# Attention with a conditioning token: the last query chunk of every even step exchanged and turned instead of scored twice

## The chip, the cores and the metric

The kernel runs on one core of one Trainium2 chip. The metric is the device time of one execution in microseconds (us). The engines have short names in the profile: PE is TensorE (PEld its weight loads), DVE VectorE, ACT ScalarE, POOL GpSimd, SP SyncE, which here only issues transfers.

## The reference

For each of 8 batch entries, x has 512 rows of 512 columns; there are 16 heads of 32 columns.

```python
Q, K, V = heads(x @ Wq.T + bq), heads(x @ Wk.T + bk), heads(x @ Wv.T + bv)
tQ, tK = heads(tokens @ Wq.T + bq), heads(tokens @ Wk.T + bk)   # one token per batch entry
cQ, cK = Q + tQ, K + tK
scores = einsum('bhqd,bhkd->bhqk', cQ, cK) / sqrt(32)
out = einsum('bhqk,bhkd->bhqd', softmax(scores), V)
return x + merge_heads(out)
```

Everything is float32.

## The kernel before, in words

**Steps.** The work is cut into T = 32 steps; step t = 4b + g does four heads (group g) of batch entry b. A step has 512 queries in four chunks of 128 (qc) and 512 keys in four chunks (kc). The main loop (L1122) runs t from 1 to 28; each turn consists of four items, V, q, k and v, numbered i = 0 to 3. The order of every engine's instructions, and of the transfers on the SP queue, is written out by hand: it is the order in which the program emits them (L260).

**Row scores.** `row_max(t, qc)` (L606) computes 128 x 512 scores of one query chunk for four heads: four matmuls of 32 rows side by side in the array (`row_scores`, L633), into four PSUM banks. VectorE reduces them to negated row maxima (L602 or, two banks at once, L644). `denominators` (L668) lets ScalarE take the exponentials, with the maximum as bias, and sum them along the row (L682). In item i of step t this is done for chunk i + 1 of step t + 1, and in the last item for chunk 0 of step t + 2. So in item i = 2 the last chunk (qc = 3) of step t + 1 is done and all its maxima are known; `held()` (L1135) then emits `split_max` (four small GpSimd instructions, L696 to L699, which split the maxima into three bf16 parts) and `turn_max` (L707), one transposing transfer on SP at L712. Its result, maxT, is what the first matmul of the next step reads.

**Two ways to weighted values.** The product with v needs the exponentials with keys on the partitions, while the row scores have queries there.
- Even steps compute the scores a second time, transposed. `exponentials(t, kc)` (L733) adds, in PSUM, the negated maxima (ones times maxT in bf16, L738) and the scores (L741), 512 queries wide, and ScalarE writes their exponentials to the arena (L752). This is done in item i for kc = i.
- Odd steps from 1 to 27 (the list BLOCKED) keep the exponentials of the rows. `exchange(t, half)` (L657) moves them between groups of 32 partitions by 16 transfers of 128 KB, 12 on SP and 4 on GpSimd's queue, and `turn_blocks` (L650) transposes them on VectorE in blocks of 32 x 32, eight instructions L655 a step. The two halves of the exchange of step t + 1 are emitted behind items 0 and 2 of the even step t; the table TURNED places the turns.

**Item V** does `weighted(t - 1)` (L813): the product of the exponentials of the step before with v (`times_v`, L754, matmuls at L763), the spreading of the sums (L800), reciprocals (L810) and `send` (L827), which turns the result on VectorE (L830), multiplies it by the reciprocals and adds the residual on GpSimd. Matmuls with 32 columns of weights run four side by side.

**Items q, k, v** project for the next batch entry. The 512 x 512 products are done by seven half-size products (Strassen and Winograd). In odd steps `four_products` (L517) does four of the seven, ScalarE copies them out, and GpSimd adds (L544, L545). In even steps `three_products` (L547) does the other three, and VectorE adds them on (L556, 557, 558). A product is 16 matmul instructions at L469.

**Order of a pair.** In an odd step PE does, per item, four row scores and then four products (or the product with v); in an even step four second scores, four row scores and three products (or the product with v). The SP queue carries, per pair and in this order: two halves of the exchange (even step), then in the odd step the store of results and the loads of x (i = 1), maxT's transfer (i = 2) and the loads of the residual xr (i = 3). Transposes of x (`turn_x`) run on VectorE in item 0 of even steps. The last three steps have code of their own behind the loop.

Of the kernel before, what the change touches and what calls it, by code (L numbers as in the profile page):

```python
# [12 lines left out]
ALU = mybir.AluOpType  # L13
# [4 lines left out]
def kernel(  # L18
# [39 lines left out]
    P = 128  # L58
# [17 lines left out]
    BLOCKED = list(range(1, T - 4, 2))  # L76

# [136 lines left out]
    def room_for_e(t, kc, pr):  # L214

        if t + 1 in BLOCKED and kc == 0 and pr == 0:
            place[0] = 8
        i = place[0]
        place[0] = (i + 1) % ROOMS
        return arena[:, i, :].rearrange("p (i s) -> p i s", s=S)  # L220

    def rows_kept(t, half):

        a = arena[:, half * HG : (half + 1) * HG, :]
        return a.rearrange("p g (c h s) -> p g c h s", c=2, h=HG)

# [290 lines left out]
    def four_products(n, b, u, dens, small, at):  # L517

        one_, two_ = banks(at), banks(at + 1)
# [24 lines left out]
        nc.gpsimd.tensor_tensor(c1, c1, twice(m1), ALU.add)  # L544
        nc.gpsimd.tensor_tensor(c22, c22, c12, ALU.add)  # L545

    def three_products(n, b, u, dens, small, at):  # L547

        dens()
        one_, two_ = banks(at[0]), banks(at[1])  # L550
        product(n, b, u, 5, one_[:, HS:])
        product(n, b, u, 4, one_[:, :HS])
        small()
        product(n, b, u, 3, two_[:, :HS])
        c1, c12, c2, c22 = parts_of(n, b, u)
        nc.vector.tensor_tensor(c12, one_[:, HS:], c12, ALU.add)  # L556
        nc.vector.tensor_tensor(c2, halves(one_), twice(c22), ALU.add)
        nc.vector.tensor_tensor(c12, two_[:, :HS], c12, ALU.add)
# [47 lines left out]
    def row_max(t, qc, hold=False, w=HG, singly=False):  # L606
# [4 lines left out]
        for j in range(HG):  # L611
            row_scores(t, qc, j, banks(w + j))
# [20 lines left out]
    def row_scores(t, qc, j, pt):  # L633
        r = slice(j * HD, (j + 1) * HD)
        nc.tensor.matmul(  # L635
# [31 lines left out]

    def denominators(t, qc, w=HG, js=range(HG)):  # L668
# [3 lines left out]
        for j in js:  # L672
            if t in BLOCKED:
                to = rows_kept(t, qc // 2)[:, :, qc % 2, j, :].rearrange(
                    "p g (c e) -> p g c e", e=BL
                )
            else:
                to = banks(w + j)
            of = banks(w + j)
            if t in BLOCKED:  # L680
                of = of.rearrange("p (c g e) -> p g c e", g=HG, e=BL)
# [51 lines left out]
    def exponentials(t, kc, at=None):  # L733

        bank = [bank_of(i) for i in at] if at else [banks(i) for i in range(HG)]
        for j in range(HG):
            r = slice(j * HD, j * HD + 3)
            nc.tensor.matmul(bank[j], onesb[r, :], maxT[t][r, :], start=True, stop=False)  # L738
        for j in range(HG):
# [4 lines left out]
                qkT["q", t][r, :],  # L744
# [9 lines left out]
    def times_v(t, kc, pt, chunks=range(NS), half=None):  # L754
        b, g = divmod(t, G)
        at = slice(0, S) if half is None else slice(half * HS, (half + 1) * HS)
        cs = slice(0, NS) if half is None else slice(half * 2, half * 2 + 2)
# [69 lines left out]
    def send(t, y_, rec):  # L827

        y = op.tile([P, NB, BL], F32, tag="res", name=f"res_{t}", bufs=1)
        nc.vector.transpose(y.rearrange("p f e -> p (f e)"), y_)  # L830
        nc.gpsimd.tensor_tensor(y, y, rec.broadcast_to([P, NB, BL]), ALU.mult)  # L831
# [139 lines left out]
    nc.gpsimd.memset(ones, 1.0)  # L971
# [113 lines left out]
    def products(t, n, blocks, hold, dens, small):  # L1085
# [3 lines left out]
        if r % 2:  # L1089
            three_products(n, b, r // 2, dens, small, (0, 3))  # L1090
            released(1, 2, 4, 5, 6, 7, 0, 3)
# [7 lines left out]
    TURNED = {(-1, 3): 1, (0, 1): 2, (0, 2): 2, (0, 3): 3}  # L1099
    turned = {1: 1}  # L1100
    turn_blocks(1, range(1))

    def turn_more(t, i):

        for u in (t - 1, t, t + 1):
            if u in BLOCKED and (t - u, i) in TURNED:
                n = turned.get(u, 0)
                turned[u] = n + TURNED[t - u, i]
                turn_blocks(u, range(n, turned[u]))

    ORDERS = {
# [10 lines left out]
    for t in range(1, T - 3):  # L1122
# [3 lines left out]
        items = ["V", "q", "k", "v"]  # L1126
        for i, item in enumerate(items):
# [7 lines left out]
            def held(i=i, hold=hold):  # L1135
                hold()
                if i == 2:
                    split_max(t + 1)
                    turn_max(t + 1)

            dens = lambda js=range(HG): denominators(*rows, w, js)
            if item in "qkv":
                products(t, item, blocks, held, dens, nothing)
# [9 lines left out]
            if i == 0 and r % 2 == 0:  # L1153
                turn_x(t + NC + 2)
                turn_x(t + NC + 3)
            if i == 0 and r == 1:
                combine_x(b + 1, 1, nc.gpsimd)
            if i == 1 and r == 0:
# [3 lines left out]
            turn_more(t, i)  # L1162
            for what in ORDERS[t % 2, i]:
                if what == "store":
                    store()
                elif what == "residual":
# [71 lines left out]

    late.append(room("late").rearrange("p g c h s -> p (g c) (h s)"))
# [155 lines left out]
```

## Time and profile before

| | before |
|---|---|
| times of the runs | 661.33, 661.98, 661.90 us; median 661.9 |
| the profiled execution | 661.48 us, its span 659.7 us |
| granted TensorE clock, mean | 0.998 |
| ACT, POOL busy | 542.4 us (82%), 337.0 us (51%) |
| share of the 16 DMA engines' span taken by SP's queue, by GpSimd's | 49.0%, 8.9% |
| moved by transfers, mean | 138 GB/s |

The span runs from the first to the last instruction of the profiled execution; the device time has 1.8 us around it. Busy is the time in which an engine has an instruction in work. In a timeline row stand the start, the length, the engine, the line, the operation, what is written and read, and how often; an "SPq" row is the issue of transfers, not their flight. In a row of a group stand after the bar the total busy time, the mean of one instruction in ns and the idle time before it. Three numbers with slashes are the least, the median and the greatest.

### The profile page before, as it was taken

Reading aid. Unit: us, or ns where it says so; the run is one execution under the profiler, and the core shown is the slowest. Engines: PE = TensorE matmul, PEld = TensorE weight load, DVE = VectorE, ACT = ScalarE, POOL = GpSimd, SP = SyncE. Lnnn points to the kernel's source line nnn. Section 1 sums busy time; section 2 is a strip of 40 time slices with the busy share of each in tenths; the row PEclk is TensorE's granted clock in tenths of the full one; section 3 lists DMA queues with packets and bytes.
Section 4 is the critical chain, followed back from the end, with each engine's and each line's share of the span. In section 5 each row is a group of like instructions: output and inputs, shape, how many; then the busy total and the mean of one; then the engine's idle time right before and its main releaser. Section 6 shows DMA issues by size and latency. Waiting matters only on the chain.

```text
span 659.7 us, 22856 instructions
## 1 busy us (share of the span) xinstructions
PE 652.0 (99%) x9096; PEld 306.3 (46%) x9096; DVE 574.8 (87%) x843; ACT 542.4 (82%) x1392; POOL 337.0 (51%) x446
## 2 busy tenths in 40 slices
PE   8999999999999999999999999999999999999996
PEld 7444444544545444444544444454544545445432
DVE  4998988989798898979989898898979888897886
ACT  2578797888979888898989889788897988889664
POOL 5642643647537464465635664464753646354340
PEclk9999999999999999999999999999999999999999
DMA  9719548385665838557483875838576572940222
GB/s 208 142 43 220 111 113 201 77 216 120 162 166 123 210 70 221 135 137 190 100 217 87 201 149 129 206 74 220 110 171 160 128 195 54 223 95 10 50 33 33
DMA packets 140815, 90.86 MB, mean 138 GB/s; under 512 B 117436, under 2 KB 126308, under 8 KB 140708
## 3 DMA queue, kind: packets, MB, share of 16 engines
q1 hardware_dynamic: 133252, 73.91, 49.0%
q0 software_dynamic: 5568, 14.95, 8.9%
q8 instruction: 72, 1.18, 0.8%
q10 hardware_dynamic: 1888, 0.52, 0.3%
q14 instruction: 35, 0.29, 0.1%
HBM read 20.27 MB, written 8.39 MB: 43 GB/s over the span
## 4 chain that ended last, share of the span: by engine, by line
PE 92%; POOL 2%; DMA 2%; SPq 1%; DVE 1%; issue 1%; ACT 0%; ACTq 0%; POOLq 0%; DVEq 0%
PE psum L469 43%; PE psum L635 19%; PE psum L763 17%; PE psum L741 8%; PE psum L738 3%; DMA w_k<-in_L_cond_Wk_dram 1%; SPq L254 1%; PE psum L1216 1%; DMA early<-in_x_dram 1%; PE psum L773 1%; PE psum L800 0%; ACT psum L682 0%; POOL wc_q L364 0%; POOL wc_q L361 0%; POOL wc_k L362 0%
## 5 line engine op out<-in xcount | busy, mean ns | idle before, releaser
L602 DVE TENSOR_REDUCE nmax<-psum 128x1 f32<-128x512 f32 x326 | 205.1, 681 | 42.1 <-PE psum L635 41.3
L682 ACT ACTIVATE psum<-psum,nmax 128x512 f32<-128x512 f32 x256 | 169.2, 665 | 47.2 <-DVE nmax L602 35.1
L752 ACT ACTIVATE arena<-psum 128x512 f32<-128x512 f32 x264 | 136.3, 603 | 30.0 <-PE psum L741 22.1
L682 ACT ACTIVATE arena<-psum,nmax 128x512 f32<-128x512 f32 x224 | 152.8, 709 | 4.9 <-issue 4.2
L635 PE MATMUL psum<-kT,qT 32*128 32x512 f32 x1024 | 150.8, 619 | 0.0
L655 DVE STREAM_TRANSPOSE blocks<-blocks 128x1024 f32<-128x1024 f32 x112 | 132.2, 1219 | 0.2 <-DMA blocks<-arena 0.2
L644 DVE TENSOR_REDUCE nmax<-psum 128x2 f32<-128x1024 f32 x87 | 105.4, 1213 | 1.1 <-PE psum L635 1.1
L831 POOL TENSOR_TENSOR res<-res,recs 128x512 f32<-128x512 f32 x30 | 31.5, 1048 | 121.3 <-DVE res L830 121.3
L666 POOL DMA_DIRECT2D blocks<-arena x112 | 55.9, 504 | 72.3 <-ACT arena L682 63.5
L635 PEld LDWEIGHTS psum<-kT,qT 32*128 32x128 f32 x1024 | 54.5, 182 | 62.8 <-issue 18.3
L763 PE MATMUL psum<-arena,v 128*32 128x512 f32 x576 | 68.5, 597 | 0.0
L741 PE MATMUL psum<-qT,kT 32*128 32x512 f32 x528 | 67.9, 587 | 0.0
L682 ACT ACTIVATION_READ_ACCUMULATOR psum<-psum,nmax 128x1 f32 x256 | 52.5, 205 | 0.0
L763 PE MATMUL psum<-blocks,v 128*32 128x256 f32 x896 | 52.1, 381 | 0.0
L682 ACT ACTIVATION_READ_ACCUMULATOR arena<-psum,nmax 128x1 f32 x224 | 50.9, 227 | 0.0
L832 POOL TENSOR_TENSOR xr<-res,xr 128x512 f32<-128x512 f32 x30 | 38.4, 1281 | 2.4
L209 POOL TENSOR_TENSOR xr<-xr,wT_q 128x512 f32<-128x512 f32 x30 | 38.4, 1280 | 0.3
L763 PEld LDWEIGHTS psum<-blocks,v 128*32 128x32 f32 x896 | 26.3, 110 | 25.0 <-ACT arena L752 10.6
L830 DVE STREAM_TRANSPOSE res<-psum 128x512 f32<-128x512 f32 x28 | 20.1, 717 | 18.9 <-issue 15.6
L469 PE MATMUL psum<-wT_v,xT 128*32 128x256 f32 x512 | 34.2, 382 | 0.0
L469 PE MATMUL psum<-wc_v,xc 128*32 128x256 f32 x512 | 33.5, 379 | 0.0
L544 POOL TENSOR_TENSOR v<-v 128x512 f32<-128x512 f32 x14 | 17.9, 1279 | 29.2 <-ACT v L532 29.2
(190 smaller groups left out, 979.9 us busy)
## 6 DMA issues: line engine op xcount, KB each, us to landing
blocks<-arena SPq DMA_DIRECT2D x336, 128.0 KB, 4.2
blocks<-arena POOLq DMA_DIRECT2D x112, 128.0 KB, 4.0
xr<-in_x_dram SPq DMA_DIRECT2D x60, 128.0 KB, 2.5
x<-in_x_dram SPq DMA_DIRECT2D x56, 128.0 KB, 2.9
out_dram<-xr SPq DMA_DIRECT2D x56, 128.0 KB, 2.6
w_q<-in_L_cond_Wq_dram SPq DMA_DIRECT2D x4, 256.0 KB
w_k<-in_L_cond_Wk_dram SPq DMA_DIRECT2D x4, 256.0 KB, 7.3
w_v<-in_L_cond_Wv_dram SPq DMA_DIRECT2D x4, 256.0 KB
```

What stands on the lines that cost most here:

```text
L209: nc.gpsimd.tensor_tensor(xr[t], xr[t], bias, ALU.add)
L469: nc.tensor.matmul(pt[r], still[:, r], moving, start=(kc == kcs[0]), stop=(kc == kcs[-1]))
L602: nc.vector.tensor_reduce(nmax[t][:, qc, j : j + 1, 0], pt, AX.X, ALU.max, negate=True)
L635: nc.tensor.matmul(pt, qkT["q", t][r, qc * P : (qc + 1) * P], qkT["k", t][r, :], start=True, stop=True,)
L644: nc.vector.tensor_reduce(nmax[t][:, qc, pr * 2 : pr * 2 + 2, 0], pt, AX.X, ALU.max, negate=True)
L655: nc.vector.transpose(e, e)
L666: queue.dma_start(to.rearrange("p c h s -> p (c h s)"), of)
L682: nc.scalar.activation(to, of, AF.Exp, bias=nmax[t][:, qc, j, :], accum_out=sums[t][:, qc, j, :],)
L741: nc.tensor.matmul(bank[j], qkT["k", t][r, kc * P : (kc + 1) * P], qkT["q", t][r, :], start=False, stop=True,)
L752: nc.scalar.activation(e[:, i, :], bank[pr * 2 + i], AF.Exp)
L763: nc.tensor.matmul(pt[j * HD : (j + 1) * HD, at], vs[b % 2][:, kc, (g * HG + j) * HD : (g * HG + j + 1) * HD], e, start=(kc == chunks[0]), ...
L832: nc.gpsimd.tensor_tensor(xr[t], y, xr[t], ALU.add)
```

## The change

Even steps from 2 to 26 (a new list QUARTERED, 13 steps) treat their last query chunk as the odd steps treat all theirs.
- `denominators` writes the exponentials of chunk 3 of these steps to the arena (`quarter_rows`). In item i = 2 of the odd step before, `exchange_quarter` moves them by 16 transfers of 32 partitions x 512 columns (64 KB), 12 on SP and 4 on GpSimd's queue. `turn_quarter` transposes them on VectorE by two instructions of 128 x 1024, behind items 0 and 1 of the even step. `weigh_quarter` multiplies them with v, 16 matmuls of 128 columns, ahead of the products of the even step's item i = 2, and its result of 128 columns is turned by itself on VectorE.
- `exponentials` and `times_v` of these steps are 384 columns wide instead of 512; `send` turns 384 columns and multiplies in two pieces.
- In that odd item `dens()` and `exchange_quarter(t + 1)` are emitted ahead of `products`, and `held()` with `split_max` and `turn_max` is called inside `products`.
- The items of even steps come as V, k, q, v, or as V, v, k, q in steps divisible by four, no longer as V, q, k, v.
- In three or one of the three projections (HELPED) `three_products` does its products in another order and leaves one of VectorE's three additions to GpSimd; where the quarter is weighed ahead of it, it adds the first product by itself.
- Row scores of odd steps are done in two matmuls of 64 queries each instead of one of 128.
- The transposes of x move from item 0 to items 1 and 2 of even steps, the turns of blocks follow a new table (as many in the same items, one of them ahead of the item's sums), one `combine_x` moves from item 1 to item 3, and the memset of `ones` moves behind the loop, since its place serves the turned quarter.

```diff
+    QUARTERED = list(range(2, T - 4, 2))
+    HELPED = ('qkv', 'q')
+    QS = S - P
...
-        nc.gpsimd.tensor_tensor(c22, c22, c12, ALU.add)
+        nc.gpsimd.tensor_tensor(c12 if n in HELPED[u] else c22, c22, c12, ALU.add)
...
+        if n in HELPED[u]:
+            product(n, b, u, 3, two_[:, :HS])
+            product(n, b, u, 4, one_[:, :HS])
+            product(n, b, u, 5, one_[:, HS:])
+            spare = room_beside(n)
+            split_of = lambda a: a.rearrange("p (c s) -> p c s", c=2)
+            nc.vector.tensor_tensor(spare, split_of(two_[:, :HS]), split_of(c22), ALU.subtract)
+            small()
...
+                nc.vector.tensor_tensor(c2, halves(one_), twice(c12), ALU.add)
+            nc.gpsimd.tensor_tensor(split_of(c12), spare, split_of(c22), ALU.add)
...
-            row_scores(t, qc, j, banks(w + j))
+            row_scores(t, qc, j, banks(w + j), 2 if row_of[0] and w == 0 else 1)
...
+    def exchange_quarter(t):
+        if t not in QUARTERED:
+            return
+        for a in range(HG):
+            for g in range(HG):
+                queue = nc.gpsimd if g in BY_POOL else nc.sync
+                of = quarter_rows()[a * BL : (a + 1) * BL, g]
+                to = quarter_blocks()[g * BL : (g + 1) * BL, a]
+                queue.dma_start(
+                    to.rearrange("p h s -> p (h s)"), of.rearrange("p h s -> p (h s)")
+                )
...
+    def turn_quarter(t, units):
...
+            e = quarter_blocks()[:, n * 2 : n * 2 + 2].rearrange("p a h s -> p a (h s)")
+            nc.vector.transpose(e, e)
...
+    def weigh_quarter(t, pt):
...
+        for kc in range(NS):
+            for j in range(HG):
+                nc.tensor.matmul(
+                    pt[j * HD : (j + 1) * HD],
+                    vs[b % 2][:, kc, (g * HG + j) * HD : (g * HG + j + 1) * HD],
+                    quarter_blocks()[:, :, j, kc * BL : (kc + 1) * BL],
+                    start=(kc == 0),
+                    stop=(kc == NS - 1),
+                )
...
+        def turn():
+            y = wT["q"][:, 0, P : 2 * P]
+            nc.vector.transpose(y, pt)
+            y_of_quarter[t] = y.rearrange("p (f e) -> p f e", e=BL)
+        return turn
...
+            elif t in QUARTERED and qc == NS - 1:
+                to = quarter_rows()[:, :, j, :].rearrange("p g (c e) -> p g c e", e=BL)
...
+        to = slice(0, QS if t in QUARTERED else S)
+        bank = [b[:, to] for b in bank]
...
-            nc.tensor.matmul(bank[j], onesb[r, :], maxT[t][r, :], start=True, stop=False)
+            nc.tensor.matmul(bank[j], onesb[r, :], maxT[t][r, to], start=True, stop=False)
...
-        items = ["V", "q", "k", "v"]
+        items = ["V", "q", "k", "v"] if blocks else ["V", "k", "q", "v"] if t % G else ["V", "v", "k", "q"]
...
             dens = lambda js=range(HG): denominators(*rows, w, js)
+            small = nothing
+            if not blocks and i == QUARTER_AT:
+                small = weigh_quarter(t, banks(0)[:, HS : HS + P])
+            if blocks and i == 2:
+                dens()
+                dens = lambda js=None: None
+                exchange_quarter(t + 1)
             if item in "qkv":
-                products(t, item, blocks, held, dens, nothing)
+                products(t, item, blocks, held, dens, small)
```

More of the change, by code (lines that the diff above doesn't have):

```diff
@@ L517, in four_products @@
     def four_products(n, b, u, dens, small, at):
+        if n != "v":
+            for g in range(2):
+                qkT[n, b * G + u * 2 + g] = pair_of(b * G + u * 2, n)[:, g, :]
         one_, two_ = banks(at), banks(at + 1)
@@ L631, in row_max, with row_scores @@
         return nothing
-    def row_scores(t, qc, j, pt):
+    def row_scores(t, qc, j, pt, parts=1):
         r = slice(j * HD, (j + 1) * HD)
+        n = P // parts
+        if parts > 1:
+            for i in range(parts):
+                nc.tensor.matmul(
+                    pt[i * n : (i + 1) * n],
+                    qkT["q", t][r, qc * P + i * n : qc * P + (i + 1) * n],
+                    qkT["k", t][r, :],
+                    start=True,
+                    stop=True,
+                )
+            return
         nc.tensor.matmul(
@@ L1165 @@
                     store()
+                elif what == "quarter":
+                    exchange_quarter(t + 1)
                 elif what == "residual":
@@ L1237, in crossed @@
         row_max_of(u, qc, 1, banks(HG + 2, 2))
+    nc.gpsimd.memset(ones, 1.0)
     late.append(room("late").rearrange("p g c h s -> p (g c) (h s)"))
```

120 lines of the change are left out of this document (97 added, 23 removed).

## The prediction

> **What bounds the kernel now.** I read the page's busy shares first.
>
> ```profile
> span 659.7 us, 22856 instructions
> ...
> PE 652.0 (99%) x9096; PEld 306.3 (46%) x9096; DVE 574.8 (87%) x843; ACT 542.4 (82%) x1392; POOL 337.0 (51%) x446
> ```
>
> TensorE (PE) is the bound at 99%. But a matmul's end is modelled, so I price its work by the distance from one start to the next. The loop repeats in pairs of steps, one odd and one even. Next I took the stretch of one pair from the view of windows.
>
> ```profile
> core 0: us, PE busy (x) PEld busy (x) DVE busy (x) ACT busy (x) POOL busy (x), PEclk, DMA share, GB/s
> 303.95:343.05 39.10, 39.10 (x565) 18.29 (x561) 35.09 (x50) 33.89 (x89) 21.19 (x28) 1.00 0.64 151
> ```
>
> A pair takes 39.10 us. VectorE has 39.10 − 35.09 = 4.0 us free in it, ScalarE 5.2, GpSimd 17.9. Last I read the timeline around the place where an odd step hands over to an even one; that is where the change puts its transfers.
>
> ```profile
> 347.71 1.14 PE L635 MATMUL psum<-kT,qT 32*128 32x512 f32 x8
> ...
> 348.78 1.07 PE L469 MATMUL psum<-xT,wT_k 128*32 128x256 f32 x16
> ...
> 352.32 0.27 POOL L699 TENSOR_TENSOR split<-rest,split 128x16 bf16<-128x16 f32 x1
> ...
> 352.57 0.20 ACT L682 ACTIVATION_READ_ACCUMULATOR psum<-psum,nmax 128x1 f32 x1
> 352.62 1.23 SPq L712 DMA_TRANSPOSE wT_v<-split  x1
> ...
> 357.04 0.39 PE L738 MATMUL psum<-wT_v,onesb 3*128 3x512 bf16 x4
> ...
> 357.26 1.03 PE L741 MATMUL psum<-qT,kT 32*128 32x512 f32 x8
> ...
> 358.12 1.10 PE L635 MATMUL psum<-kT,qT 32*128 32x512 f32 x8
> ```
>
> The odd step's third item (i = 2) starts at 347.71. The read of its fourth exponential's sum is over at 352.77, say 352.8. Just before, at 352.59, GpSimd has split the row maxima into three bf16 parts, and at 352.62 SyncE (SP) issues the transfer that transposes them into maxT (L712). The even step's first matmul (L738) reads maxT at 357.04. The row of L712 has the time to landing:
>
> ```profile
> DMA to landing us min/median/max: 2.4/2.4/2.5
> ```
>
> So maxT is there at 352.62 + 2.4 = 355.0, and its slack is 2.0 us. Nobody waits for it today.
>
> **The change part by part.** Narrower second scores: L738 starts 0.22 us before L741, and L741 0.86 us before L635, so an item's second scores cost 1.08 us of PE. With 384 of 512 columns a quarter goes, 0.27 us an item, and an even step has four items: −1.08 us a pair. ScalarE's 16 exponentials shrink as well, but ScalarE isn't the bound.
>
> The fourth chunk's product with v moves from the odd step's V item into the even step's third item. Columns stay equal (3/4 in one place, 1/4 in the other), but it now takes 32 short matmuls of 128 columns. The nearest row is a burst of 32 of 64 columns:
>
> ```profile
> 28.25 0.63 PE L870 MATMUL psum<-wT_k,early 128*32 128x64 f32 x32
> 28.70 0.61 PE L469 MATMUL psum<-xT,wT_q 128*32 128x256 f32 x8
> ```
>
> The 32 hold PE for 28.70 − 28.25 = 0.45 us, half of what L741's eight of 512 columns hold it for. 128 columns should then take about 0.9 us, as much as leaves the V item: I take 0 (−0.05 to +0.1).
>
> The odd steps' row scores are cut into halves of 64 queries: 16 matmuls for 8. No row shows such a shape. At worst the halves pass one after the other, +0.86 us for each of four items; at best the change of shape behind them gets cheaper, and there only 1.07 − 0.86 = 0.21 us an item can be saved. I take 0, by the burst of short matmuls above.
>
> The order of k, q, v and the sums on GpSimd:
>
> ```profile
> PEld psum L635 <- DVE kT L558: 6.6, 14, 0.7
> ...
> PEld psum L635 <- DVE qT L557: 5.3, 13, 0.4
> ```
>
> PE's row scores wait for VectorE's sums 6.6 + 5.3 = 11.9 us over 14 pairs, 0.85 us a pair. The new order puts k ahead of q and drops one VectorE sum in four of six items, but it also puts more on VectorE behind them:
>
> ```profile
> L655 DVE STREAM_TRANSPOSE blocks<-blocks 128x1024 f32<-128x1024 f32 x112 | 132.2, 1219 | 0.2 <-DMA blocks<-arena 0.2
> ...
> L556 DVE TENSOR_TENSOR qT<-psum,qT 128x256 f32<-128x256 f32 x14 | 5.8, 415 | 0.0
> ```
>
> Added in a pair: two turns of the quarter at 132.2/112 = 1.18 us, and a turn of 128 columns (an estimate of 0.3, twice its share of the 1.18 us of 1024 columns), of which the narrower turn in send gives half back. Removed: two sums of 0.41. VectorE comes to 35.1 + 2.36 + 0.15 − 0.83 = 36.8 us a pair. It stays below PE, with less room. I set what the order saves against what VectorE's load brings: 0, with 0.85 us either way. GpSimd's additions (four DMA issues, two sums, one more product a pair, some 4 us) fit into its 17.9 free us. The moved memset, and the turns of x that move by an item or two, cost nothing beside the PE work of those items.
>
> **The wait that it adds** is the large term. In program order `exchange_quarter(t + 1)` stands in the odd step's third item ahead of `products`, whose first act is `held()`, hence `split_max` and `turn_max`. Twelve of the quarter's 16 transfers go through SP and four through GpSimd, and they need all four exponentials. So behind a wait until 352.8, SP issues twelve transfers, and only then L712, which is ready to go today at 352.62; the four loads of xr queue behind. Who waits for L712 is PE. What does an issue cost SP?
>
> ```profile
> L666 SPq DMA_DIRECT2D blocks<-arena x336: 507/593/2265, 49.8 to 577.0; - x168
> ...
> L246 SPq DMA_DIRECT2D early<-in_L_cond_Wq_dram x2: 407/414/420, 0.7 to 1.2; - x2
> ...
> L303 SPq DMA_DIRECT2D early<-in_cond_dram x4: 272/293/332, 3.1 to 4.1; - x4
> ```
>
> The exchange of today, 128 KB each over 32 partitions, costs 0.59 us (0.63 with the gap to the next); 64 KB from HBM (L246) 0.41; 4 KB (L303) at least 0.27. The quarter's are 64 KB over 32 partitions: I take 0.50 with its gap, between the first two, and keep 0.27 and 0.63 as ends. L712 is then issued at 352.8 + 12 × 0.50 = 358.8, lands at 361.2, and L738 runs at 361.3 instead of 357.04: PE stands still for 4.3 us. GpSimd's side is earlier: four issues at the same 0.50 and the split, four instructions like L699's of 0.27, are over at 355.9. The ends give 1.4 us and 5.7 us. The even V item needs maxT with its first matmul, and PE takes its work in order: there is nothing to put into the gap.
>
> What would be late next: the turn of the quarter behind the even V item needs the first half landed. SP has issued that by 355.8, and today's twice as large transfers land so long after their issue (the page's last column, median):
>
> ```profile
> blocks<-arena SPq DMA_DIRECT2D x336, 128.0 KB, 4.2
> ```
>
> That is 360.0, and the turn comes behind a V item that begins at 361.3: in time.
>
> The landing of 2.4 us was measured behind no other transfer. The Trainium skill, "DMA: Bandwidth & Descriptors", section "Queues, rings and completion order", says that a transfer's semaphore lands only after every earlier write of the same DMA engine, across its queues. By that rule maxT couldn't land before the quarter's last transfers; with the exchange's 4.2 us in the place of 2.4 the stall would be up to 1.8 us longer, 23 us over 13 pairs. No row of before has L712 behind a burst.
>
> **Sum.** 39.10 − 1.08 + 4.3 = 42.3 us a pair, +3.2 us. Steps 2 to 26 are quartered: 13 pairs, +42 us. The profiled execution took 661.5 us for a span of 659.7, so 701.5 of span and 703.5 us; the median shown, 661.9, lies 0.4 above that execution.
>
> **Rivals.** (1) The other side: maxT isn't late enough to matter. The stall equals the gain of 1.08 us when the twelve issues take 2.0 + 1.1 = 3.1 us, 0.26 us each; below this the change wins. For it: the split of the exchange over two queues already shortens SP's part. Against it: the cheapest row is 0.27 us for 4 KB. With no stall at all, 661.5 − 13 × 1.08 = 647.5 us; 0.15 for faster, and 0.03 for about break-even.
>
> (2) Cheap issues, and VectorE instead. If an issue costs 0.27 to 0.35 us the stall is 1.4 to 2.4 us, 666 to 679 us. VectorE then decides from below: 36.8 us and the 4.0 us that it can't fill today make 40.8 us a pair, 661.5 + 13 × 1.7 = 684 us. Under the forecast's 42.3 us this is hidden. 0.12.
>
> (3) The clock falls in the gaps. The kernel's last matmuls in the timeline, the granted clock behind them in the windows (third column from the end), and the kernel's first matmuls:
>
> ```profile
> 655.18 0.44 PE L1345 MATMUL psum<-ident,late 128*128 128x128 f32 x2 [0.48 <-DVE late L1343]
> ...
> 657.00:658.00 1.00, 0.00 (x0) 0.00 (x0) 0.00 (x0) 0.00 (x0) 0.00 (x0) 0.82 1.27 197
> 658.00:659.00 1.00, 0.00 (x0) 0.00 (x0) 0.00 (x0) 0.00 (x0) 0.00 (x0) 0.50 0.18 27
> ...
> 1.06 5.05 PE L900 MATMUL psum<-onesb 128*128 128x128 bf16 x48 [1.06 <-DVE onesb L277]
> ```
>
> It halves at about 657.6, 2.0 us after PE fell idle; the forecast's gaps are twice that. For the way back there is the kernel's start: 48 matmuls of 128 columns take 5.05 us, 0.105 each, where L738's 512 columns hold PE for 0.22 us, 0.055 for 128. So PE was slow for some 5 us there. If half clock lasted 5 us behind each gap it would cost 2.5 us, 13 times: 736 us. Against it: one fall in one place is all the evidence, and the loop has no gap to test it. The Trainium skill, "TensorE: Matmul & The Clock Gate", section "Part 1: The HAM clock gate", has the clock halve after an idle window of about 3.4 us and return after a busy one; by an estimate from that page it would be 1.7 us a gap, 726 us. The trace's fall came earlier than that window. 0.16.
>
> (4) The row halves pass one after the other: +0.86 us in three items whose cost shows, the fourth hides in the gap: 703.5 + 13 × 2.6 = 737 us. Nothing speaks for it but the missing row. 0.04.
>
> **How the numbers follow.** The forecast, 703.5 us, has 0.50; its own range, with issues of 0.37 to 0.63 us, is 684 to 722 us. The whole range, 655 to 732 us, takes in rival 2, break-even, the less gainful end of rival 1 and the lower part of rival 3, and leaves out some 0.2. Faster by over 0.2% (about what can be told from no change here) 0.15, within it 0.03, slower 0.82.
>
> **What would show it.** The forecast: a pair of some 42 us, L712 issued about 6 us behind the last exponential of the odd third item, and PE's L738 (another line number there) waiting about 4 us for wT_v<-split in each of 13 even steps. The score groups' starts 0.27 us closer, or not. Rival 2: the same wait, shorter, and row scores that wait for VectorE. Rival 3: a granted clock under 1.0 in the windows behind the gaps. Rival 4: 1.9 us from an odd item's row scores to its products, where it is 1.07. I am wrong if L738 waits for nothing, above all if the issues on SP cost a quarter of a microsecond.

## The result and the profile after

The changed kernel takes 772.6 us (median of five runs, 771.4 to 773.9), the kernel before 661.9 us: 1.168 times as long [1.167, 1.169]. The forecast was 703.5 us with a range up to 732. The direction was right, and the size was 69 us short.

The page of the changed kernel (the profiled execution took 773.9 us) has these lines. The last is the group of the even steps' first matmuls, with TensorE's idle time ahead of it in its last column.

```profile
span 772.0 us, 25326 instructions
...
PE 677.3 (88%) x9960; PEld 327.9 (42%) x9960; DVE 596.8 (77%) x854; ACT 527.8 (68%) x1392; POOL 380.8 (49%) x539
...
L844 PE MATMUL psum<-wT_v,onesb 3*128 3x384 bf16 (+1 forms) x264 | 25.4, 375 | 85.1 <-DMA wT_v<-split 85.1
```

TensorE was busy 99% of the time and is now busy 88%. L844 is what L738 was, and it waits 85.1 us for the transfer of maxT, where the prediction had 13 × 4.3 = 56. The timeline at one handover from an odd to an even step (L680: row scores in halves; L786: the exponentials of rows; L730: the quarter's transfers; L816: maxT's; L847 and L688: second scores and row scores of the even step):

```profile
407.97 1.11 PE L680 MATMUL psum<-kT,qT 32*64 32x512 f32 x16
...
412.87 0.20 ACT L786 ACTIVATION_READ_ACCUMULATOR arena<-psum,nmax 128x1 f32 x1
413.09 8.61 SPq L730 DMA_DIRECT2D arena<-arena  x12
416.34 0.27 POOL L803 TENSOR_TENSOR split<-rest,split 128x16 bf16<-128x16 f32 x1
421.80 1.23 SPq L816 DMA_TRANSPOSE wT_v<-split  x1
424.30 0.51 PE L844 MATMUL psum<-wT_v,onesb 3*128 3x384 bf16 x4 [6.99 <-DMA wT_v<-split]
424.59 1.49 PE L847 MATMUL psum<-qT,kT 32*128 32x384 f32 x8
425.87 1.92 PE L688 MATMUL psum<-kT,qT 32*128 32x512 f32 x8
...
431.92 0.34 PE L844 MATMUL psum<-wT_v,onesb 3*128 3x384 bf16 x4
```

The fourth exponential's sum is read by 413.07, 5.1 us behind the item's start, as the prediction placed it. SP issues twelve transfers from 413.09 to 421.70. The parts of maxT have been ready since 416.61, but L816 is issued at 421.80 only, and TensorE waits 6.99 us. Behind the gap the same groups are longer than usual: L844 takes 0.51 us here and 0.34 one item later. The view of windows says why: first the whole pair, then one microsecond at a time, the granted clock in the third column from the end.

```profile
407.97:455.98 48.01, 41.02 (x629) 19.79 (x625) 36.95 (x53) 32.60 (x89) 23.57 (x34) 0.93 0.60 147
421.00:422.00 1.00, 0.00 (x0) 0.00 (x0) 0.00 (x0) 0.00 (x0) 1.00 (x1) 1.00 0.50 125
422.00:423.00 1.00, 0.00 (x0) 0.00 (x0) 0.00 (x0) 0.00 (x0) 0.10 (x1) 0.53 0.29 72
...
425.00:426.00 1.00, 1.00 (x12) 0.47 (x8) 0.00 (x0) 0.00 (x0) 0.00 (x0) 0.50 1.17 264
...
428.00:429.00 1.00, 1.00 (x20) 0.50 (x16) 1.00 (x2) 0.46 (x1) 0.00 (x0) 0.56 0.00 0
429.00:430.00 1.00, 1.00 (x24) 0.60 (x20) 1.00 (x2) 0.99 (x4) 0.00 (x0) 1.00 0.00 0
```

This pair takes 48.0 us where it took 39.1; the difference between the pair and TensorE's busy time is just the one gap, 48.01 − 41.02 = 6.99. It is one of the longer gaps: the thirteen are 6.5 us on average (85.1/13), and a pair is 8.5 us longer on average (110.7/13). The clock halves at about 422.0, 4.7 us after TensorE fell idle (424.30 − 6.99 = 417.3), and stays halved until 428.9, 4.6 us behind the restart. So rival 3 came on top of the forecast, not in its place.

The trace's record of the granted clock has the same at all thirteen gaps. Each low stretch lasts 6.83 us, 4.0 to 6.3 us of it behind the restart (4.8 on average), and they begin 47.78 us apart, whatever the gap. The gaps of the last three handovers are about 1 us shorter, 5.8 to 5.9 us, but the pairs between them only 0.2 to 0.4 us (47.4 and 47.5 us from restart to restart, 47.7 on average before): there the clock stayed low for 5.6 to 6.3 us behind the restart.

The twelve issues are the largest surprise. The view of line L730, minimum, median and maximum in ns:

```profile
L730 SPq DMA_DIRECT2D arena<-arena x156: 507/589/1949, 79.3 to 658.4; - x156
```

The median is 0.59 us, as for the odd steps' transfers of twice the size. In the burst above the twelve take 0.52, 0.59, 0.60, 0.60, 0.59, 1.70 and six times 0.59 us, with 0.05 between: 0.72 on average, against the 0.50 taken. In ten of the thirteen bursts one issue is long, 0.99 to 1.95 us; in the last three, none is. Over all thirteen, a burst holds maxT's issue back by 8.31 us, 0.69 for each transfer. And maxT's flight, the line to landing in the view of its tile:

```profile
DMA to landing us min/median/max: 2.4/2.4/2.5
```

It is what it was before, although twelve transfers stand ahead of it. The stretch of up to 1.8 us by the completion rule of the Trainium skill ("DMA: Bandwidth & Descriptors", "Queues, rings and completion order") didn't come. That does not speak against the rule: the quarter's transfers on SP landed 2.0 us after their issue (median), and the last of them, where the trace has its landing, 1.3 us after maxT's issue and so ahead of maxT.

### The profile page after: what moved, and what is told of

It reads as the page before. It is cut to its first block, busy times and chain, and to the rows that moved or that the text cites. A ratio compares the mean times of both kernels' runs of the same rounds, so it can differ in the third digit from the quotient of the medians.

```text
span 772.0 us, 25326 instructions
## 1 busy us (share of the span) xinstructions
PE 677.3 (88%) x9960; PEld 327.9 (42%) x9960; DVE 596.8 (77%) x854; ACT 527.8 (68%) x1392; POOL 380.8 (49%) x539
## 4 chain that ended last, share of the span: by engine, by line
PE 57%; POOL 17%; DMA 7%; issue 7%; DVE 6%; SPq 3%; ACT 3%; ACTq 0%; DVEq 0%; POOLq 0%
PE psum L486 17%; PE psum L871 13%; PE psum L688 11%; PE psum L847 7%; DMA wT_v<-split 4%; PE psum L680 3%; POOL arena L730 3%; PE psum L844 3%; DVE nmax L697 2%; PE psum L755 2%; POOL v L564 2%; SPq L730 2%; POOL kT L564 2%; DVE nmax L644 2%; POOL xr L213 1%
## 5 line engine op out<-in xcount | busy, mean ns | idle before, releaser
L786 ACT ACTIVATE arena<-psum,nmax 128x512 f32<-128x512 f32 x276 | 187.2, 687 | 36.5 <-DVE nmax L644 14.3
L858 ACT ACTIVATE arena<-psum 128x384 f32<-128x384 f32 (+1 forms) x264 | 114.1, 519 | 133.7 <-PE psum L847 131.6
L786 ACT ACTIVATE psum<-psum,nmax 128x512 f32<-128x512 f32 x204 | 134.3, 660 | 37.7 <-DVE nmax L644 27.5
L708 DVE STREAM_TRANSPOSE blocks<-blocks 128x1024 f32<-128x1024 f32 x112 | 132.1, 1217 | 0.0
L688 PE MATMUL psum<-kT,qT 32*128 32x512 f32 x576 | 106.3, 698 | 0.1
L946 POOL TENSOR_TENSOR res<-res,recs 128x512 f32<-128x512 f32 (+1 forms) x30 | 28.6, 954 | 149.6 <-DVE res L939 149.5
L844 PE MATMUL psum<-wT_v,onesb 3*128 3x384 bf16 (+1 forms) x264 | 25.4, 375 | 85.1 <-DMA wT_v<-split 85.1
L719 POOL DMA_DIRECT2D blocks<-arena x112 | 55.7, 503 | 50.2 <-ACT arena L786 38.9
L847 PE MATMUL psum<-qT,kT 32*128 32x384 f32 (+1 forms) x528 | 65.6, 574 | 0.0
L680 PE MATMUL psum<-kT,qT 32*64 32x512 f32 x896 | 63.6, 613 | 0.0
L688 PEld LDWEIGHTS psum<-kT,qT 32*128 32x128 f32 x576 | 44.9, 209 | 31.0 <-issue 11.3
L871 PE MATMUL psum<-arena,v 128*32 128x384 f32 (+1 forms) x576 | 57.4, 520 | 0.0
L844 PEld LDWEIGHTS <-onesb 3*128 3x128 bf16 x264 | 6.7, 92 | 115.3 <-DMA wT_v<-split 91.3
L786 ACT ACTIVATION_READ_ACCUMULATOR arena<-psum,nmax 128x1 f32 x276 | 55.6, 201 | 0.0
L585 POOL TENSOR_TENSOR qT<-wT_q,qT 128x256 f32<-128x256 f32 x14 | 10.2, 726 | 65.3 <-DVE qT L584 65.3
L786 ACT ACTIVATION_READ_ACCUMULATOR psum<-psum,nmax 128x1 f32 x204 | 40.9, 200 | 0.0
```

The source lines that it names most:

```text
L680: nc.tensor.matmul(pt[i * n : (i + 1) * n], qkT["q", t][r, qc * P + i * n : qc * P + (i + 1) * n], qkT["k", t][r, :], start=True, stop=True,)
L688: nc.tensor.matmul(pt, qkT["q", t][r, qc * P : (qc + 1) * P], qkT["k", t][r, :], start=True, stop=True,)
L708: nc.vector.transpose(e, e)
L719: queue.dma_start(to.rearrange("p c h s -> p (c h s)"), of)
L786: nc.scalar.activation(to, of, AF.Exp, bias=nmax[t][:, qc, j, :], accum_out=sums[t][:, qc, j, :],)
L844: nc.tensor.matmul(bank[j], onesb[r, :], maxT[t][r, to], start=True, stop=False)
```

## The experiments

**The theory** after this reading: a pair grew by some 8.5 us because (a) maxT stands behind twelve issues, (b) the clock halves in the gap, (c) the narrower scores didn't pay. **The rivals**: the time goes with the bytes of the quarter, so that any place for them costs the same; VectorE's added turns or the row halves carry a part. Medians in us; each ratio is against runs of the kernel before on the same chip.

| kernel | median | lowest to highest | ratio to before [95%] |
|---|---|---|---|
| e1_turn_first | 683.6 | 678.9–684.1 | 1.031 [1.028, 1.035] |
| e2_filled | 752.5 | 748.9–755.6 | 1.137 [1.133, 1.141] |
| e3_half_bytes | 745.6 | 744.0–746.5 | 1.126 [1.124, 1.128] |
| e4_halves_alone | 661.1 | 660.8–662.1 | 0.999 [0.998, 1.000] |
| e5_no_sp_quarter | 670.3 | 668.0–671.7 | 1.012 [1.009, 1.015] |
| e6_no_turn | 679.0 | 677.6–685.0 | 1.028 [1.022, 1.033] |
| e7_not_helped | 688.4 | 683.3–696.5 | 1.038 [1.029, 1.047] |
| e8_narrow | 657.7 | 657.4–658.5 | 0.994 [0.992, 0.996] |
| e9_no_quarter | 663.6 | 663.1–664.1 | 1.002 [1.001, 1.003] |
| e10_all_on_sp | 758.1 | 743.4–761.2 | none worked out, since the runs spread |
| e11_quarter_later | 681.4 | 678.9–686.4 | 1.031 [1.026, 1.036] |
| e12_narrow_exps | 656.6 | 656.0–656.7 | 0.992 [0.991, 0.993] |
| e13_turn_later | 669.8 | 667.5–671.2 | 1.012 [1.009, 1.015] |
| e14_residual_later | 666.8 | 666.1–667.0 | 1.007 [1.006, 1.009] |

### What the gap costs, and what makes it

**e1_turn_first**: maxT's transfer ahead of the quarter's.

```diff
             def held(i=i, hold=hold):
                 hold()
-                if i == 2:
+                if i == 2 and not blocks:
                     split_max(t + 1)
...
                 dens = lambda js=None: None
+                split_max(t + 1)
+                turn_max(t + 1)
                 exchange_quarter(t + 1)
```

> The changed kernel with one difference: the split of the row maxima and maxT's transposing transfer are emitted ahead of the quarter's exponentials and transfers in the odd step's third item. Theory (maxT stands behind twelve issues on SP, and TensorE's clock falls in the gap that follows): the pair of 48.0 us loses the 7.0 us of the gap and some 2.1 us of half clock behind it, 38.9 us a pair, about 659 us in all (650 to 668). Rival (the quarter's transfers delay the even step whatever their place, through VectorE's turns or the exchange behind them): the time stays above 720 us.

It takes 683.6 us: 89 us of the 110.7 are gone, by the order of two calls alone. The wait is the cause of these 89 us. But 22 us stay, which neither case of the expectation covers; the next group of experiments is about them.

**e2_filled**: the changed kernel, with TensorE kept busy in the gap by 110 matmuls that nobody uses.

```diff
+            if t in QUARTERED and i == 0:
+                for _ in range(110):
+                    nc.tensor.matmul(banks(0)[:, :P], onesb, onesb, start=True, stop=True)
```

> The changed kernel with 110 extra bf16 matmuls of 128 columns on TensorE ahead of each quartered step's first matmul; they compute nothing that is used and take some 6 us, less than the gap. Theory (the half clock behind the gap costs by itself some 2 us a pair): granted clock 1.00 behind the gap, about 27 us less than the changed kernel, 745 us. Rival (behind the gap TensorE would wait for others anyway, so the clock costs nothing): 772 us, or more by whatever the fill takes.

752.5 us, 20.1 us less than the changed kernel. At the handover shown (L1281: the filling; L816 as above) TensorE runs through, and the V item behind it takes 417.47 − 412.04 = 5.43 us, where the changed kernel has 431.92 − 424.30 = 7.62:

```profile
405.79 6.32 PE L1281 MATMUL psum<-onesb 128*128 128x128 bf16 x110
409.45 1.23 SPq L816 DMA_TRANSPOSE wT_v<-split  x1
...
412.04 0.34 PE L844 MATMUL psum<-wT_v,onesb 3*128 3x384 bf16 x4
...
417.47 0.34 PE L844 MATMUL psum<-wT_v,onesb 3*128 3x384 bf16 x4
```

The clock therefore costs 2.2 us in the item behind a gap, and 20.1/13 = 1.5 us a pair show in the time. The other 0.7 goes into a longer handover: the filling takes 6.3 us, and at 11 of the 13 handovers TensorE then still waits for maxT, 11.8 us in all or 0.9 a pair, where the changed kernel stands still for 6.5.

**e3_half_bytes**: each transfer of the quarter moves two of four heads, 32 KB; the exchange of the other two heads' numbers is left out.

```diff
-                    to.rearrange("p h s -> p (h s)"), of.rearrange("p h s -> p (h s)")
+                    to[:, 0:2].rearrange("p h s -> p (h s)"), of[:, 0:2].rearrange("p h s -> p (h s)")
```

> The changed kernel, but each of the quarter's 16 transfers moves only two of the four heads (32 KB instead of 64 KB; the rest of the data is left out, so the result is not the reference's). Theory (an issue on SP costs 0.6 us for the form of the transfer, not for its bytes): the same twelve issues, the same gap of 7 us, 771 to 774 us. Rival (bytes set the cost): the gap halves to about 3 us and the time falls below 725 us.

745.6 us, which neither theory gives. The view of its line L730 and its timeline settle it:

```profile
L730 SPq DMA_DIRECT2D arena<-arena x156: 507/589/1655, 77.5 to 632.5; - x156
```

```profile
399.92 8.02 SPq L730 DMA_DIRECT2D arena<-arena  x12
400.18 0.69 ACT L786 ACTIVATE arena<-psum,nmax 128x512 f32<-128x512 f32 x1 [0.28 <-DVE nmax L697]
...
410.53 0.51 PE L844 MATMUL psum<-wT_v,onesb 3*128 3x384 bf16 x4 [4.66 <-DMA wT_v<-split]
```

An issue costs the same 0.59 us with half the bytes. But the transfers now need only two of the four exponentials and start ahead of the third, 1.7 us earlier against the row scores than in the changed kernel. The gap falls from 6.99 to 4.66 us by that (on average from 6.5 to 60.9/13 = 4.7, 24 us in all), and 27 us go. The experiment changed two things; the row of the issues is its answer, the time isn't. It shows one thing more: gaps of 4.1 to 5.4 us, the length that was forecast, halved the clock at all thirteen handovers.

**e4_halves_alone**: the kernel before, with the row scores of odd steps in halves of 64 queries.

```diff
-            row_scores(t, qc, j, banks(w + j))
+            row_scores(t, qc, j, banks(w + j), 2 if row_of[0] and w == 0 else 1)
...
-    def row_scores(t, qc, j, pt):
+    def row_scores(t, qc, j, pt, parts=1):
```

> The kernel before with one part of the change alone: the row scores of the odd steps in two matmuls of 64 queries. Theory (the halves run side by side): an odd item stays at 4.64 to 4.66 us, 660 to 663 us. Rival (they pass one after the other): +0.86 us an item, about 710 us.

661.1 us, 0.9991 of before: the halves run side by side, as taken.

### What is left when maxT is first

In e1 short and long pairs alternate, and at 8 handovers TensorE still waits for maxT, 9.2 us in all. The timeline of a long pair (L719: the odd step's exchange; L708: VectorE's turn of its blocks; L584 and L585: the last sum of q on VectorE and the one handed to GpSimd; L680: the odd step's row scores):

```profile
384.59 12.40 SPq L719 DMA_DIRECT2D blocks<-arena  x15
...
390.70 1.25 DVE L708 STREAM_TRANSPOSE blocks<-blocks 128x1024 f32<-128x1024 f32 x1 [0.82 <-DMA blocks<-arena]
...
392.38 0.69 DVE L584 TENSOR_TENSOR qT<-psum,qT 128x512 f32<-128x512 f32 x1
393.16 0.72 POOL L585 TENSOR_TENSOR qT<-wT_q,qT 128x256 f32<-128x256 f32 x1 [5.07 <-DVE qT L584]
...
394.40 1.94 PE L680 MATMUL psum<-kT,qT 32*64 32x512 f32 x16
```

Three candidates: SP's queue (a short pair lasts 38.7 us, and in the pair shown the issues fill about 37: 19.3 for the 24 of the exchange, 2.3 for the store, 3.2 for x, 1.2 for maxT, 8.2 for the quarter, 2.8 for xr), VectorE's load, the sums on GpSimd. **e5_no_sp_quarter** leaves out SP's twelve transfers, **e6_no_turn** the two turns of the quarter; the fourth chunk's product then works on old data, or on data that were not turned. **e7_not_helped** gives the sums back to VectorE. In this order:

```diff
+                if g not in BY_POOL:
+                    continue
...
-            nc.vector.transpose(e, e)
+            pass
...
-    HELPED = ('qkv', 'q')
+    HELPED = ('', '')
```

> The kernel of e1_turn_first (683.6 us) without the twelve transfers of a quarter that SyncE issues; GpSimd's four stay, so that the quarter product of the even steps works on old data (the result is not the reference's). Theory A, SyncE's queue is what is left: its load falls from about 37 of 38.7 us a pair to 29, the exchange of the odd step's halves is issued on time, and the slow pairs of 42 us come down to 38.8: 658 to 668. Theory B, VectorE's load (36.9 of 41.9 us in a slow pair) or the sums handed to GpSimd: the time stays within 678 to 686.

> The kernel of e1_turn_first (683.6 us) without VectorE's two turns of the quarter per even step, 2.36 us a pair (the result is not the reference's). Theory B, VectorE is what is left: up to 2.36 us for each of 13 pairs, about 31 us, goes, 653 to 670. Theory A, SyncE's queue: 679 to 685.

> The kernel of e1_turn_first (683.6 us) with no sum handed to GpSimd: VectorE does about two more sums of 0.45 us a pair, the first scores no longer wait for GpSimd. Theory C, the wait for GpSimd's sum (2.2 us in the slow pairs, 6 times) is what is left: 665 to 672. Theory B, VectorE's load: 690 to 698. Theory A, SyncE's queue: 681 to 686.

They took 670.3, 679.0 and 688.4 us. SP's twelve transfers account for 13 us of the 22; 670.3 lies just above what theory A allowed. Taking 31 us of work from VectorE gives 4.6, within the spread of the runs: its load is not the bound. Without the helped sums (two runs at 683, two at 693 and 697) it gets no faster, so theory C falls. In e5 two pairs of 42 us remained, behind a late maxT: it landed 4.6 us after its issue there, and 4.8 in e1, in place of 2.4. In both, GpSimd issues its four transfers of the quarter 0.2 or 0.4 us behind maxT. That gave theory F, tried with **e9_no_quarter** (none of the sixteen; old data again), **e10_all_on_sp** (GpSimd's four on SP) and **e11_quarter_later** (the exchange called behind the item's products: the same order on SP, GpSimd's four 2 to 3 us later); in this order:

```diff
-        for a in range(HG):
+        for a in range(0):
...
-                queue = nc.gpsimd if g in BY_POOL else nc.sync
+                queue = nc.sync
...
-                exchange_quarter(t + 1)
...
-        (1, 2): [],
+        (1, 2): ["quarter"],
```

> The kernel of e1_turn_first (683.6 us) without any of the quarter's sixteen transfers, GpSimd's four too; the even steps' quarter product works on old data (the result is not the reference's). Without SyncE's twelve it took 670.3, and the transposing transfer of the maxima still landed after 4.6 us where it had taken 2.4 before. Theory F, it is GpSimd's four transfers, issued 1 us behind it, that stretch its landing: it lands after 2.4 again, the two slow pairs of 42.4 us go, 13 pairs of 39.1 to 39.4: 660 to 666. Rival, the landing was stretched by the reads of x ahead of it: landing 4.6 again and 668 to 672.

> The kernel of e1_turn_first (683.6 us) with GpSimd's four transfers of the quarter issued by SyncE too, sixteen on SyncE. Theory A, SyncE's queue is the larger part: its load goes from about 37 to 39.7 us a pair, more than the 38.8 of a fast pair, and the time rises to 690 to 700. Theory F, the landing stretched by GpSimd's transfers is the larger part: it lands after 2.4 us and the time falls to 674 to 681.

> The kernel of e1_turn_first (683.6 us) with the quarter's exchange called at the end of the odd step's third item: the order on SyncE's queue is the same, only GpSimd's four transfers move behind its sums of the projection, some 4 us, and so behind the landing of the maxima. Theory F: landing 2.4 to 3 us, and 676 to 681. Rival, SyncE's own transfers stretch the landing, or the load of its queue is all: 682 to 686.

With no transfer of the quarter it is 663.6 us, 0.2% above before. The median landings were 3.0 (e9), 2.4 (e10) and 3.9 us (e11). That does not show GpSimd's four to be the cause. The traces have the landing of only four to six of a run's fifteen transposing transfers; e9's lie between 2.4 and 4.4 us without the four, and in e7, where the four stand 0.4 us behind maxT, three of five are 3.0 or 3.1. What stretches the landing stays open. And it is worth little: e11's time can't be told from e1's. e10 lost 60 to 78 us by four more issues on SP, which no expectation had. Its timeline shows a chain that e1 has in small:

```profile
428.69 9.15 SPq L719 DMA_DIRECT2D blocks<-arena  x13
...
433.26 1.25 DVE L708 STREAM_TRANSPOSE blocks<-blocks 128x1024 f32<-128x1024 f32 x1 [4.46 <-DMA blocks<-arena]
434.43 0.39 DVE L578 TENSOR_TENSOR wT_q<-psum,qT 128x256 f32<-128x256 f32 x1
434.95 0.69 DVE L584 TENSOR_TENSOR qT<-psum,qT 128x512 f32<-128x512 f32 x1
...
435.73 0.72 POOL L585 TENSOR_TENSOR qT<-wT_q,qT 128x256 f32<-128x256 f32 x1 [8.65 <-DVE qT L584]
...
436.50 3.31 PE L680 MATMUL psum<-kT,qT 32*64 32x512 f32 x16 [3.11 <-POOL qT L585]
```

SP's queue starts the odd step's exchange late, since xr and the quarter stand ahead of it. VectorE reaches its first turn of these blocks, which the change's new table puts ahead of the last item's sums, and waits 4.46 us for them. Behind the turn stand q's sums, behind these GpSimd's, behind that the row scores, and TensorE falls idle. The clock then falls here too (0.50 from 438 to 442 in the view of windows). This chain was tried with **e13_turn_later** (e11 with that turn behind the sums) and **e14_residual_later** (e13 with the reads of xr behind the exchange's first half); first e13's edit, which it makes for (2, 3) as well, then e14's:

```diff
-        (0, 3, 'm'): 'b',
+        (0, 3, 'e'): 'b',
...
-        (1, 3): ["residual"],
-        (0, 0): [0],
+        (1, 3): [],
+        (0, 0): [0, "residual"],
...
-                    if 3 < t + 1 <= T - 4:
-                        load_residual(t + 1)
+                    if 3 < t <= T - 4:
+                        load_residual(t)
```

> The kernel of e11_quarter_later (681.4 us) with VectorE's first turn of the odd step's blocks moved from ahead of the even step's last product sums to behind them. Theory G, the late blocks hold the turn, and the turn holds q's sums, GpSimd's helped sum and the row scores: the row scores no longer wait, about 1.2 us for each of 13 pairs goes, 664 to 670. Rival, VectorE only does the same work later and the odd step's maxima wait in their turn, or the blocks' lateness moves on to the weighted sums: 677 to 684.

> The kernel of e13_turn_later with SyncE's four reads of the residual (2.2 to 3.5 us a pair) moved from ahead of the odd step's exchange to behind its first half, so that the exchange starts some 3 us earlier. If lateness of SyncE's queue is still what costs behind the moved turn, it falls below e13_turn_later by 2 us or more; if the moved turn has taken the lateness off the path, the two agree within 1.5 us.

669.8 and 666.8 us: theory G holds (e13 is 11.6 us below e11), and the lateness of SP's queue was worth 3 us more behind it. The same place in the timelines of e11 and e14:

```profile
387.92 1.25 DVE L708 STREAM_TRANSPOSE blocks<-blocks 128x1024 f32<-128x1024 f32 x1 [1.13 <-DMA blocks<-arena]
...
389.61 0.69 DVE L584 TENSOR_TENSOR qT<-psum,qT 128x512 f32<-128x512 f32 x1
...
390.38 0.72 POOL L585 TENSOR_TENSOR qT<-wT_q,qT 128x256 f32<-128x256 f32 x1 [5.38 <-DVE qT L584]
...
391.31 2.25 PE L680 MATMUL psum<-kT,qT 32*64 32x512 f32 x16
```

```profile
381.24 0.69 DVE L584 TENSOR_TENSOR qT<-psum,qT 128x512 f32<-128x512 f32 x1 [0.57 <-PE psum L486]
381.84 1.23 DVE L708 STREAM_TRANSPOSE blocks<-blocks 128x1024 f32<-128x1024 f32 x1
...
384.87 1.46 PE L680 MATMUL psum<-kT,qT 32*64 32x512 f32 x16
```

The turn no longer waits, q's sum is ahead of it, and the group of row scores is through in 1.46 us instead of 2.25.

### What the narrower scores are worth

**e8_narrow** is the kernel before with the second scores of steps 2 to 26 at 384 columns; **e12_narrow_exps** has their exponentials narrowed too. The last chunk's second scores are left out in these steps. The last line pair of the diff is e12's.

```diff
+        to = slice(0, S - P if t in range(2, T - 4, 2) else S)
...
-            nc.tensor.matmul(bank[j], onesb[r, :], maxT[t][r, :], start=True, stop=False)
+            nc.tensor.matmul(bank[j][:, to], onesb[r, :], maxT[t][r, to], start=True, stop=False)
...
-                nc.scalar.activation(e[:, i, :], bank[pr * 2 + i], AF.Exp)
+                nc.scalar.activation(e[:, i, to], bank[pr * 2 + i][:, to], AF.Exp)
```

> The kernel before with the second scores of the even steps 2 to 26 narrowed to 384 columns and nothing else changed (the last query chunk's exponentials are then taken of old numbers, and the result is not the reference's). The prediction's term stands: 1.08 us less for each of 13 pairs, 14 us, 648 (645 to 652), since TensorE sets the time of the kernel before. Rival: ScalarE's exponentials, which stay 512 wide, set the pace of these items, and it stays at 658 to 662.

> The kernel of e8_narrow (657.7 us) with the exponentials of the even steps narrowed to 384 columns as well (0.60 to about 0.50 us each, sixteen a pair; the last query chunk's are left out, and the result is not the reference's). In e8_narrow TensorE's next products wait for the last of these exponentials to give a bank free. If ScalarE's pace is what took the gain, the full 1.08 us a pair comes out: 647 to 650. If another engine's pace takes it (VectorE's maxima, the copies): 655 to 658.

657.7 and 656.6 us: 4.1 and 5.3 us, 0.3 and 0.4 a pair, where 1.08 was expected. The even step's second item before, then in e8 (ones, second scores, row scores, products):

```profile
401.90 0.39 PE L738 MATMUL psum<-wT_v,onesb 3*128 3x512 bf16 x4
402.13 1.03 PE L741 MATMUL psum<-qT,kT 32*128 32x512 f32 x8
402.99 1.02 PE L635 MATMUL psum<-kT,qT 32*128 32x512 f32 x8
403.94 1.07 PE L469 MATMUL psum<-xT,wc_q 128*32 128x256 f32 x16
```

```profile
399.73 0.34 PE L739 MATMUL psum<-wT_v,onesb 3*128 3x384 bf16 x4
399.90 0.81 PE L742 MATMUL psum<-qT,kT 32*128 32x384 f32 x8
400.55 1.28 PE L635 MATMUL psum<-kT,qT 32*128 32x512 f32 x8
401.76 1.07 PE L469 MATMUL psum<-xT,wc_q 128*32 128x256 f32 x16
```

The row scores start 0.27 us earlier, as expected: 0.82 us behind the item's start in place of 1.09. But they now take 1.28 us, and the products begin 2.03 us behind the item's start, where it was 2.04. So a busy TensorE can hide a wait: the group of row scores starts earlier and ends when it did before. Of the even step's items only the third got shorter, from 5.08 to 4.83 us; the first stayed at 5.78, the second went from 4.77 to 4.76, and what follows up to the next even step from 23.46 to 23.45. The rival, that ScalarE's exponentials set this pace, is not borne out: narrowing them brought 1.1 us of the missing 10. What holds the row scores was not tried. In the item shown, the weights of three of the four heads' row scores are loaded 0.96 us behind the item's start in the kernel before, in e8 and in e12 alike, 0.05 us after VectorE has turned the weighted values out of PSUM (L830 of the kernel before).

## Why the prediction was wrong, point by point

- **The added wait**: its mechanism, its place and its times up to the first issue were right. The term that failed is "the quarter's are 64 KB over 32 partitions: I take 0.50", between a row of 128 KB and one of 64 KB from HBM. e3 shows that bytes don't enter: 0.59 us at 32, 64 and 128 KB over 32 partitions. With the gap it is 0.64, beyond the end of 0.63 that was kept, and with the long issues 0.69 on average. 12 × (0.69 − 0.50) = 2.3 us, and the gap became 6.5 on average instead of 4.3. The trace of the kernel before had the larger figure. Its exchange of a pair, two bursts of twelve with 1.3 us between them, takes 18.79 us in the line below, which leaves 0.73 for each issue; the prediction went by the median of single issues.

```profile
363.23 18.79 SPq L666 DMA_DIRECT2D blocks<-arena  x24
```

- **The clock** (rival 3, at 0.16) was priced as an alternative, though it follows from the forecast's own gap, as e3 shows. It costs 2.2 us a pair by e2, and half of the 4.8 us at half clock is 2.4. The prediction's 2.5 by rows was close; its 1.7 by the page of the Trainium skill was too little.
- **Narrower second scores**: −1.08 was taken, 0.3 to 0.4 was found (e8, e12). TensorE's share of 99% was read as if every shortened matmul would show.
- These three come to 2.2 + 2.2 + 0.7 = 5.1 us a pair, 66 us in 13 pairs, of the 69 that the forecast was short.
- **A slip**: by the prediction's own sum an issue of 0.37 us gives 681 us, not 684; nothing hangs on it.
- **Row halves at 0**: right (e4). **The quarter's product at 0**: no run tried it alone; about 0.5 us a pair at most, by the 7 us below, if those two runs may be set against each other.
- **Order, sums and VectorE's load at 0**: the sum above leaves 0.2 us a pair for all of them in the changed kernel. Rival 2's floor of 684 us was not VectorE's load, as e6 shows, so that e1's 683.6 agrees with it by chance.
- **Rival 1** priced a harmless maxT at 647.5 us. e1 takes most of that wait away (9.2 of 85.1 us are left) and reaches 683.6. What was missing: SP's queue runs nearly full and starts the odd step's exchange late, and VectorE's turn of the blocks, in its new place ahead of the sums, hands that on to TensorE. The prediction asked which transfers L712 stands behind, but not what stands behind xr. With four things moved (maxT's turn, the quarter's exchange, the turn of the blocks, the reads of xr) the kernel comes to 666.8 us (e14); that is 3.2 us above e9, which has no transfer of the quarter but only the first of the four moves.
- No version that does the whole work was clearly faster than the kernel before. The narrower scores bring 5.3 us as placed here (e12), and e9 without any transfer is at 663.6, so the rest of the change costs 7 us against them, if the two add up.

## What to carry to other kernels

Count the issues of an in-order queue by their number, not by their bytes, take their price from a whole burst and not from the median of one, and list everything that stands behind a new burst, one step further than the first victim. A gap of several microseconds on TensorE has a second price in the clock: add it to the forecast, not beside it. And a saving on the engine that is 99% busy has to be tried at its place: here most of it only lengthened the group of instructions behind.

## What the runs showed of the hardware

- Issuing a transfer of 32 partitions between places of the arena cost SP 0.59 us (median) at 32, 64 and 128 KB. In ten of the thirteen bursts of the changed kernel one issue took 0.99 to 1.95 us; why was not tried.
- The granted clock halved 3.9 to 5.3 us after TensorE fell idle in the changed kernel's thirteen gaps, for 6.83 us each time; in e3 it halved for 3.41 or 6.83 us. Gaps of 2.19 us in e1 and of 2.03 and 2.16 us in e5 were enough for a fall, of 3.41 us. At the end of the kernel before it halved 2.0 us behind the last matmul, but TensorE had been busy for only 1.5 of the 3 us before 656. The Trainium skill, "TensorE: Matmul & The Clock Gate", section "Part 1: The HAM clock gate", has an idle window of about 3.4 us; the changed kernel's gaps agree with it, those of e1 and e5 were shorter.
- The transposing transfer of maxT landed in 2.4 us behind twelve transfers of its own queue (six handovers of the changed kernel have the landing). In e1, e5 and e6, with four of GpSimd's issued 0.2 or 0.4 us after it, the medians were 4.6 to 4.8, but 3.0 in e7, which has them 0.4 us after it; that difference is not settled.
- Row scores cut into two matmuls of 64 queries cost nothing measurable (0.9991).
